# A residual block-attention kernel: the first tile of Wo transposed by VectorE in 32x32 blocks, two of its column quarters loaded through GpSimd's queue, with smaller units and a re-ranked plan

## The chip, the cores and the metric

One core of a Trainium2 chip runs the whole program. The metric is the device time in microseconds of one execution; the median of three is 150.2 us (149.64 to 150.42). The profile shows one of the executions (149.81 us), whose span from the first to the last instruction is 148.0 us. Below, x "at 44.6" means 44.6 us after the start of that span. The engines are TensorE (PE), VectorE (DVE), ScalarE (ACT), GpSimd (POOL) and SyncE (SP), which issues nearly all the transfers.

## What is computed

The input x is (8, 512, 1024) float32. The reference, cut to what matters, with NUM_BLOCKS = 8:

```python
block_repr = inputs.reshape(B, n_blocks, block_size, H).sum(axis=2)
keys = jnp.einsum('bnh,kh->bnk', block_repr, Wk)
keys = keys / jnp.sqrt(jnp.mean(keys * keys, axis=-1, keepdims=True) + EPS) * rms_weight
attn = softmax(jnp.einsum('bnh,h->bn', keys, query_vectors[layer_idx]))
attended = jnp.einsum('bn,bnh->bh', attn, block_repr)
proj = jnp.einsum('bh,kh->bk', attended, Wo)          # one vector for each batch element
y = inputs + proj
out = x + layernorm(y) * ln_gamma + ln_beta           # x is the same array as inputs
```

Each of the 8 batch elements has 512 rows of 1024 numbers. Their block sums pass through Wk to scores, the scores through a softmax to weights, and the weighted block sums through Wo to one vector, which is added to all 512 rows. Every row is then normalised, scaled, shifted and added to its input. 16.8 MB of x come in and as much goes out; the two weights are 4 MB each.

## The kernel before, in words

**Groups, rows and units.** The batch is worked in four groups of two elements (`GROUPS`). A group has four x tiles of 128 partitions by two rows by 1024 (1 MB each), eight "rows" (128x1024) in all; the program has 32 rows, 0 to 31. Rows are gathered into units (`UNITS`), and a unit shares one set of statistics.

**The start.** The weights come as four 1 MB tiles each, in the order of `LOADS` (k for Wk, x, o for Wo). TensorE transposes each tile with 16 matmuls against the identity (L400, two groups of eight, tile `pt`), and ScalarE copies the result from PSUM into `wkT` or `woT` (L407). The products of the first group with Wk and Wo are done quarter by quarter as the weight tiles arrive (L448, `first_keys`, `first_values`). Keys give the softmax weights through a chain of short operations on ScalarE, VectorE and TensorE (L571 to L617). The last step is the "spread" (L504 for the first group, L654 for the others): it puts the projected vector of each batch element on all partitions, in PSUM tile `pb`.

**A row's way.** y: VectorE adds `pb` to the row in place and sums it (L705). sq: ScalarE squares it with an accumulated sum (L713). When a unit's squares are there, GpSimd makes rs, the reciprocal deviation, and the statistics (L727, L728, L732, and L737 where a row is on VectorE). TensorE turns the statistics (pl, L742), and ScalarE or VectorE copies them to `lt` (L749; `LT_ACT` lists the units that ScalarE takes). For most rows ScalarE makes A = gam*rs + 1 (L762) and GpSimd multiplies the row by it (v, L767). For the rows in `ON_DVE`, TensorE makes that factor in PSUM (pA, L773) and VectorE multiplies (vd, L779). TensorE makes the additive part b from `lt` and `tab` (L794), VectorE adds it (out, L807), and SyncE stores the tile of two rows (L814).

**Order.** Nothing is scheduled at run time. Each step is handed to a `Plan` with an engine, an estimated cost, needs and a rank, and the plan simulates the engines and writes the instructions in the order of the simulated starts. The ranks `R` and the constants at the top decide that order; each engine then runs its list strictly in turn and waits where an operand or a buffer is missing. Buffers: 13 x tiles (`XBUFS`, shared with the weight tiles before they are transposed), two A tiles, two `lt`, one statistics tile, and single PSUM banks s1, s2, b0, b1 and pb.

Of the kernel before, what the change touches and what calls it, by code (L numbers as in the profile page):

```python
# [23 lines left out]
F32 = mybir.dt.float32  # L24
# [5 lines left out]
P = 128  # L30
# [2 lines left out]
NBLK = 8  # L33
GROUPS = (2, 2, 2, 2)
XBUFS = 13
ABUFS = 2
STATS = 1
LT_ACT = (1, 5, 7, 8, 9)

R = dict(  # L40
    y=3.0, sq=2.5, A=7.0, v=-6.0, out=0.5, vd=-1.0, scale=0.0, lt=-20.0, pl=-200.0, b=-250.0,
    pA=5.0, att=-10.0, hold=50.0, frac=0.8,
)
ON_DVE = (25, 27, 29, 31)
LOADS = "kxxxxkkkoooo"
W_DVE = ()
EV_DVE = ()
UNITS = (4, 4, 2, 4, 2, 4, 4, 4, 4)


class Plan:
# [4 lines left out]
    MB = 2.56  # L56
    LAND = 2.0
    BEGIN = 2.0

    def __init__(self, buffers):  # L60
        self.steps = []
        self.buffers = buffers

    def add(self, engine, cost, emit, needs=(), rank=0.0, moved=0.0, takes=None, gives=None):
        needs = [n for n in needs if n is not None]
        self.steps.append((engine, cost, emit, needs, rank, moved, takes, gives))
        return len(self.steps) - 1

# [45 lines left out]
    def emit(self):  # L114
        self.end, start, done = self.order()
        self.start, self.done = dict(enumerate(start)), dict(enumerate(done))
        for i in sorted(range(len(start)), key=lambda i: (start[i], i)):
            self.steps[i][2]()


@with_exitstack
def block_attn_resid_kernel(
# [11 lines left out]
    nc = tc.nc  # L134
    B, S, H = x.shape
    HC = H // P
    HALF = 512
    QU = H // 4
# [15 lines left out]
    ps = ctx.enter_context(tc.tile_pool(name="ps", bufs=1, space=bass.MemoryType.PSUM))  # L154
    ctx.enter_context(tc.manual_schedule())
    plan = Plan(dict(s1=1, s2=1, b=1, A=ABUFS, lt=2))
    for g in sizes:
        for n in range(STATS):
            plan.buffers[f"stat{g}_{n}"] = 1
# [115 lines left out]
    groups = []  # L275
    at = 0
# [12 lines left out]
    def load_w(which, s):  # L289
        def emit():  # L290
            if (which, s) in W_DVE:

                t = xp.tile([P, RT * 4, QU], F32, tag="x", name=f"w{which}_{s}")
                for j in range(4):
                    nc.sync.dma_start(out=t[32 * j : 32 * j + 32], in_=wq_v[which][s, :, :, bass.ts(j, QU)])
            else:
                t = xp.tile([P, RT, H], F32, tag="x", name=f"w{which}_{s}")
                nc.sync.dma_start(out=t, in_=w_v[which][s])
            stage[which, s] = t

        staged[which, s] = plan.add(SP, 0.5 if (which, s) in W_DVE else 0.35, emit, rank=-500 + len(loads), moved=1.0)

    def load_x(G, t, needs):
        def emit():
# [70 lines left out]
    def transpose_w(which, s):  # L375
        out_ = []
        if (which, s) in W_DVE:
            for c in range(0, HC, 2):
                def there_and_back(c=c):
                    t = stage[which, s].rearrange("p t (k c) -> p c t k", c=HC)  # L380
                    nc.vector.transpose(
                        (wkT, woT)[which][:, c : c + 2, bass.ts(s, QU)].rearrange("p c (t k) -> p c t k", k=32),
                        t[:, c : c + 2],
                    )

                out_.append(plan.add(DVE, 0.62, there_and_back, [staged[which, s]], -300 + which))
            halves[which, s] = out_
            frees.append(out_)
            return out_
        for h4 in range(HC // 4):  # L390
            n = turn[0]
            turn[0] += 1
            tag = ("b0", "b1", "pb")[n % 3] if n < 12 else ("b0", "b1")[n % 2]
            hold = {}

            def there(h4=h4, tag=tag, hold=hold):
                pt = ps.tile([P, 4, RT * P], F32, tag=tag, name=f"pt_{which}_{s}_{h4}")
                for c in range(4):
# [54 lines left out]
    def first_keys(G, T, columns, blkT):  # L453

        rank = -299.8
        parts = []
        for s in range(4):
            last = plan.add(PE, 0.97, lambda s=s: quarter(T, "keys", wkT, columns, s), [blkT, *halves[0, s]], rank, takes="s2")

            def e_part(s=s):  # L460
                if s == 0:
                    T["parts"] = chain.tile([P, 4, QU], F32, tag="parts", name="parts")
                nc.scalar.copy(T["parts"][:, s, :], T["po"])

            parts.append(plan.add(ACT, 0.37, e_part, [last], rank, gives="s2"))

        def e_keys():
            T["keys"]["po"] = ps.tile([P, QU], F32, tag="s1", name="keys0")
            for s in range(4):
                nc.tensor.matmul(T["keys"]["po"][32 * s : 32 * s + 32, :], diag4, T["parts"][:, s, :], start=True, stop=True)  # L470

        return plan.add(PE, 0.55, e_keys, parts, rank)

    def first_values(G, T, columns, share, blkT, rank):


        rank = -299.5
        T["w0"] = chain.tile([P, P], F32, tag="w", name="w0")

        def e_w0():  # L480
            nc.scalar.activation(T["w0"], weigh0, AF.Identity, scale=T["own"])
            T["pick"] = chain.tile([P, 2, P], F32, tag="pickw", name="pickw0")
            nc.scalar.activation(flat(T["pick"]), flat(pick0), AF.Identity, scale=T["own"])

        w0 = plan.add(ACT, 0.65, e_w0, [share], rank)
        vals = []
        for s in range(4):
            last = plan.add(
                PE, 0.97, lambda s=s: quarter(T, "values", woT, columns, s), [blkT, *halves[1, s]], rank, takes="s2"
            )  # L490

            def e_val(s=s):
                if s == 0:
                    T["val0"] = work.tile([P, 4, QU], F32, tag="A", name="val0")
                nc.scalar.copy(T["val0"][:, s, :], T["po"])

            vals.append(plan.add(ACT, 0.37, e_val, [last], rank, takes=None if s else "A", gives="s2"))
# [334 lines left out]
    for G in groups:  # L832
        attend(G)
        rows = [define_unit(u) for u, U in enumerate(units) if place[U["k0"]][0] is G]
        for _ in range(2):
            for unit_ in rows:
                next(unit_, None)
    plan.emit()
    return plan

# [29 lines left out]
```

## Time and profile before

| what | busy us | share of the span |
|---|---|---|
| TensorE matmuls | 122.6 | 83% |
| ScalarE | 101.2 | 68% |
| VectorE | 93.5 | 63% |
| GpSimd | 82.0 | 55% |
| the hardware queue of SyncE | | 70.2% of 16 DMA engines |

The shares are averages over stages with different limits. In the first third TensorE and the loads work and the other engines mostly wait; from 44.6 us on, VectorE, ScalarE and GpSimd share the rows. The costliest groups are v on GpSimd (28 of 2377 ns, 65.8 us), out (32 of 1216 ns, 38.2) and y (32 of 1213 ns, 37.6) on VectorE, sq (32 of 1143 ns, 36.6) and A (28 of 1142 ns, 31.8) on ScalarE. GpSimd's first statistic waits 47.0 us for its first squares. Page and trace name a line, an engine, an operation and the tiles written and read; in brackets stands the idle time of the engine just ahead, and what ended it.

### The profile page before, as it was taken

The page shows a single profiled execution, that of the slowest core. Times are in us where ns is not written, and L with a number is a line of the kernel's source. Part 1 is how long each engine was busy: PE and PEld are TensorE (multiplying, and loading weights), DVE is VectorE, ACT ScalarE, POOL GpSimd, SP SyncE. Part 2 cuts the span into 40 slices and gives each one's busy share as a digit, 9 for nine tenths or more (in the row PEclk, how much of TensorE's full clock was granted, in tenths as well). Part 3 has the DMA queues.
Part 4 walks back from the last instruction along what each step waited for, and adds up shares of the span by engine and source line. Part 5 has one row for each costly group of instructions (what it writes and reads, how often), then busy time and mean ns, then how long its engine had stood idle before and what let it go on. Part 6 is the DMA issues. An engine that isn't in the chain of part 4 may idle for free.

```text
span 148.0 us, 3021 instructions
## 1 busy us (share of the span) xinstructions
PE 122.6 (83%) x1176; PEld 66.2 (45%) x1176; DVE 93.5 (63%) x178; ACT 101.2 (68%) x160; POOL 82.0 (55%) x80
## 2 busy tenths in 40 slices
PE   0499989999999799969799999978894694998920
PEld 0465568768757344336354365425441212333400
DVE  6201010013109973769999899999797999694960
ACT  0352329678935999776999999998969999533000
POOL 7200000000000049999499999999999999978000
PEclk9999999999999999999999999999999555555555
DMA  4999999999999991258477795742562634657275
GB/s 131 437 408 425 398 408 411 410 415 422 416 414 418 421 403 38 106 206 354 190 248 317 292 361 210 288 193 91 213 263 91 279 133 164 283 210 301 91 317 215
DMA packets 6830, 42.15 MB, mean 285 GB/s; under 512 B 656, under 2 KB 672, under 8 KB 2720
## 3 DMA queue, kind: packets, MB, share of 16 engines
q1 hardware_dynamic: 6784, 41.95, 70.2%
q8 instruction: 9, 0.15, 0.4%
q14 instruction: 5, 0.04, 0.1%
q10 hardware_dynamic: 32, 0.02, 0.0%
HBM read 25.18 MB, written 16.78 MB: 283 GB/s over the span
## 4 chain that ended last, share of the span: by engine, by line
PE 44%; DVE 24%; issue 11%; ACT 8%; POOL 6%; DMA 3%; DVEq 1%; POOLq 0%; ACTq 0%
DVE x L705 14%; PE pt L400 12%; DVE x L807 8%; PE b L794 6%; POOL x L767 5%; PE pA L773 4%; ACT sq L713 4%; DMA w<-in_L_cond_Wk_dram 3%; ACT A L762 3%; PE bs L545 3%; PE keys L448 3%; PE values L448 3%; PE keys L433 3%; PE values L433 3%; PE pb L504 2%
## 5 line engine op out<-in xcount | busy, mean ns | idle before, releaser
L767 POOL TENSOR_TENSOR x<-x,A 128x1024 f32<-128x1024 f32 x28 | 65.8, 2377 | 4.8 <-ACT A L762 4.7
L705 DVE SCALAR_TENSOR_TENSOR x<-x,pb 128x1024 f32<-128x1024 f32 x32 | 37.6, 1213 | 7.1 <-PE pb L504 7.1
L807 DVE TENSOR_TENSOR x<-x,b 128x1024 f32<-128x1024 f32 x32 | 38.2, 1216 | 6.0 <-POOL x L767 5.3
L713 ACT ACTIVATE sq<-x,ysum 128x1024 bf16<-128x1024 f32 x32 | 36.6, 1143 | 2.5 <-DVE x L705 2.1
L794 PE MATMUL b<-tab,lt 32*128 32x512 f32 x128 | 33.1, 805 | 3.5 <-DVE x L807 2.7
L762 ACT ACTIVATE A<-gam,rs 128x1024 f32<-128x1024 f32 x28 | 31.8, 1142 | 5.8 <-POOL rs L728 3.5
L727 POOL TENSOR_SCALAR ssq<-ssq 128x4 f32<-128x4 f32 (+1 forms) x9 | 2.1, 228 | 48.2 <-ACT sq L713 47.7
L400 PE MATMUL pt<-ident,w 128*128 128x128 f32 x128 | 18.1, 299 | 5.9 <-DMA w<-in_L_cond_Wk_dram 5.9
L400 PEld LDWEIGHTS pt<-ident,w 128*128 128x128 f32 x128 | 16.5, 198 | 8.3 <-issue 8.3
L545 PE MATMUL bs<-x,blk 128*32 128x256 f32 x256 | 15.9, 386 | 1.4 <-issue 1.4
L794 PEld LDWEIGHTS b<-tab,lt 32*128 32x128 f32 x128 | 9.6, 226 | 16.3 <-DVE x L807 8.5
L433 PE MATMUL keys<-wkT,blkT 128*32 128x256 f32 x192 | 11.6, 382 | 2.3 <-DVE blkT L556 2.3
L433 PE MATMUL values<-woT,blkT 128*32 128x256 f32 x192 | 11.6, 381 | 0.5 <-ACT lt L749 0.5
L545 PEld LDWEIGHTS bs<-x,blk 128*32 128x32 f32 x256 | 7.7, 112 | 8.7 <-issue 4.2
L407 ACT COPY wkT<-pt 128x1024 f32<-128x1024 f32 x8 | 7.7, 1015 | 4.7 <-PE pt L400 4.7
L575 DVE SCALAR_TENSOR_TENSOR junk<-keys,qw 128x256 bf16<-128x256 f32 x4 | 1.7, 423 | 14.0 <-ACT junk L571 14.0
L773 PE MATMUL pA<-tabf,lt 32*128 32x512 f32 x16 | 8.1, 1108 | 2.4 <-DVE x L705 1.9
L407 ACT COPY woT<-pt 128x1024 f32<-128x1024 f32 x8 | 7.9, 1016 | 2.0 <-PE pt L400 2.0
L433 PEld LDWEIGHTS keys<-wkT,blkT 128*32 128x32 f32 x192 | 5.6, 109 | 8.0 <-DVE blkT L556 3.8
L728 POOL TENSOR_TENSOR rs<-ssq,power 128x4 f32<-128x4 f32 (+1 forms) x9 | 8.6, 961 | 0.8
L433 PEld LDWEIGHTS values<-woT,blkT 128*32 128x32 f32 x192 | 5.8, 110 | 4.9 <-issue 0.8
L779 DVE TENSOR_TENSOR x<-x,pA 128x1024 f32<-128x1024 f32 x4 | 4.9, 1221 | 3.1 <-PE b L794 3.1
(97 smaller groups left out, 112.5 us busy)
## 6 DMA issues: line engine op xcount, KB each, us to landing
x<-in_x_dram SPq DMA_DIRECT2D x16, 1024.0 KB, 14.1
out_dram<-x SPq DMA_DIRECT2D x16, 1024.0 KB, 4.1
w<-in_L_cond_Wk_dram SPq DMA_DIRECT2D x4, 1024.0 KB, 5.0
w<-in_L_cond_Wo_dram SPq DMA_DIRECT2D x4, 1024.0 KB, 19.4
gb<-in_cond_dram ACTq DMA_DIRECT2D x1, 4.0 KB
gb<-n_L_cond_rms_weight_dram ACTq DMA_DIRECT2D x1, 4.0 KB
gb<-in_L_cond_ln_gamma_dram ACTq DMA_DIRECT2D x1, 4.0 KB
gb<-in_L_cond_ln_beta_dram ACTq DMA_DIRECT2D x1, 4.0 KB
```

What stands on the lines that cost most here:

```text
L400: nc.tensor.transpose(pt[:, c, r * P : (r + 1) * P], stage[which, s][:, r, bass.ds(4 * h4 + c, P, step=HC)], ident)
L407: (nc.vector.tensor_copy if n in EV_DVE else nc.scalar.copy)(dst, hold["pt"])
L433: nc.tensor.matmul(hold["po"][32 * j : 32 * j + 32, :], lhs(c), wT[:, c, bass.ts(j, QU)], start=(c == 0), stop=(end and c == HC - 1),)
L448: nc.tensor.matmul(T["po"][32 * j : 32 * j + 32, :], columns(2 * j + c), wT[:, 2 * j + c, bass.ts(s, QU)], start=(c == 0), stop=(c == 1),)
L545: nc.tensor.matmul(T["bs"][32 * j : 32 * j + 32, :], blk[g], G["x"][t][:, r, bass.ts(j, QU)], start=(t == 0 and r == 0), stop=(t == G["til ...
L705: nc.vector.scalar_tensor_tensor(x_row(k), x_row(k), 1.0, G["pb"], ALU.mult, ALU.add, accum_out=U["sum"][:, i : i + 1])
L713: nc.scalar.activation(junk, x_row(k), AF.Square, bias=U["sum"][:, i : i + 1], scale=-float(H), accum_out=U["ssq"][:, i : i + 1],)
L762: nc.scalar.activation(U["A", k], gam, AF.Identity, bias=1.0, scale=U["rs"][:, k - k0 : k - k0 + 1])
L767: nc.gpsimd.tensor_tensor(x_row(k), x_row(k), U.pop(("A", k)), ALU.mult)
L773: nc.tensor.matmul(U["pA", k][:, i, :], U["lt"][lo : lo + 32, pair, :], tabf[lo : lo + 32, :], start=True, stop=True,)
L794: nc.tensor.matmul(U["b", pair][r][:, i, :], U["lt"][lo : lo + 32, pair, :], G["T"]["tab"][lo : lo + 32, :], start=True, stop=True,)
L807: nc.vector.tensor_tensor(x_row(k), x_row(k), flat(U["b", pair][k % RT]), ALU.add)
```

## The change

The stated aim is to take the first tile of Wo off TensorE. The tile is loaded in another layout, 32 partitions for each quarter of its columns, and VectorE transposes it in 32x32 blocks straight into `woT`. SyncE loads two of the quarters, GpSimd's queue the other two, which it issues once the second tile of Wk has landed. With it come: a third A buffer, paid for by letting `parts` use the buffers of `tab`; 13 units instead of 9; five rows on VectorE instead of four, spread over the program; eight units' `lt` on ScalarE instead of four units' in effect; other ranks; and a filler, a matmul whose result nobody reads, written into each gap that the plan sees on TensorE after the last group's spread. In the changed program there are 21 of them: runs of six, two, one, eight, and four single ones. An empty table of rank corrections (`NUDGE`) changes nothing.

```diff
-ABUFS = 2
+ABUFS = 3
-LT_ACT = (1, 5, 7, 8, 9)
+LT_ACT = (4, 6, 7, 8, 9, 10, 11, 12)
 R = dict(
-    y=3.0, sq=2.5, A=7.0, v=-6.0, out=0.5, vd=-1.0, scale=0.0, lt=-20.0, pl=-200.0, b=-250.0,
-    pA=5.0, att=-10.0, hold=50.0, frac=0.8,
+    y=2.0, sq=3.0, A=5.5, v=-3.0, out=-6.5, vd=-1.0, scale=-10.0, lt=10.0, pl=-20.0, b=-20.0,
+    pA=-250.0, att=-20.0, hold=1000.0, frac=1.0,
 )
-ON_DVE = (25, 27, 29, 31)
+ON_DVE = (10, 18, 27, 29, 31)
-W_DVE = ()
+W_DVE = ((1, 0),)
-UNITS = (4, 4, 2, 4, 2, 4, 4, 4, 4)
+UNITS = (2, 2, 4, 4, 4, 2, 2, 2, 2, 2, 2, 2, 2)
...
+            if self.steps[i][0] == "PE" and self.filler:
+                if at is not None:
+                    for _ in range(int((start[i] - at - 0.2) / self.FILL)):
+                        self.filler[1]()
+                if at is not None or i == self.filler[0]:
+                    at = done[i]
...
-                for j in range(4):
+                for j in range(2):
                     nc.sync.dma_start(out=t[32 * j : 32 * j + 32], in_=wq_v[which][s, :, :, bass.ts(j, QU)])
...
+        def others():
+            for j in range(2, 4):
+                nc.gpsimd.dma_start(
+                    out=stage[which, s][32 * j : 32 * j + 32], in_=wq_v[which][s, :, :, bass.ts(j, QU)]
+                )
+            i = plan.add(POOL, 2.0, others, [loads[len(loads) - 3], staged[which, s]], rank=-500)
...
-                out_.append(plan.add(DVE, 0.62, there_and_back, [staged[which, s]], -300 + which))
+                out_.append(plan.add(DVE, 1.07, there_and_back, [staged[which, s]], -300 + which))
...
-                    T["parts"] = chain.tile([P, 4, QU], F32, tag="parts", name="parts")
-                nc.scalar.copy(T["parts"][:, s, :], T["po"])
+                    T["parts", s // 2] = chain.tile([P, HALF], F32, tag="tab", name=f"parts{s // 2}", bufs=2)
+                nc.scalar.copy(T["parts", s // 2][:, bass.ts(s % 2, QU)], T["po"])
...
+    def e_fill():
+        idle = ps.tile([P, QU], F32, tag="s1", name="idle")
+        nc.tensor.matmul(idle, ident, gam[:, :QU], start=True, stop=True)
+    plan.filler = groups[-1]["spread"], e_fill
```

The branch for `W_DVE` is in the kernel before as well, but with an empty list nothing takes it. On the other engines the order moves with the ranks. In the changed program VectorE makes three of the four transposes, then the first group's dot product, then the fourth; TensorE takes Wo's second tile right after the first group's keys, and one block sum of the second group goes ahead of the first group's last spread matmul.

More of the change, by code (lines that the diff above doesn't have):

```diff
@@ L35 @@
 XBUFS = 13
-ABUFS = 2
+ABUFS = 3
 STATS = 1
-LT_ACT = (1, 5, 7, 8, 9)
+LT_ACT = (4, 6, 7, 8, 9, 10, 11, 12)
 R = dict(
-    y=3.0, sq=2.5, A=7.0, v=-6.0, out=0.5, vd=-1.0, scale=0.0, lt=-20.0, pl=-200.0, b=-250.0,
-    pA=5.0, att=-10.0, hold=50.0, frac=0.8,
+    y=2.0, sq=3.0, A=5.5, v=-3.0, out=-6.5, vd=-1.0, scale=-10.0, lt=10.0, pl=-20.0, b=-20.0,
+    pA=-250.0, att=-20.0, hold=1000.0, frac=1.0,
 )
-ON_DVE = (25, 27, 29, 31)
+ON_DVE = (10, 18, 27, 29, 31)
 LOADS = "kxxxxkkkoooo"
-W_DVE = ()
+W_DVE = ((1, 0),)
 EV_DVE = ()
-UNITS = (4, 4, 2, 4, 2, 4, 4, 4, 4)
+NUDGE = {}
+UNITS = (2, 2, 4, 4, 4, 2, 2, 2, 2, 2, 2, 2, 2)
 class Plan:
@@ L58 @@
     BEGIN = 2.0
+    FILL = 0.36
     def __init__(self, buffers):
@@ L62, in __init__ @@
         self.buffers = buffers
+        self.nudge, self.filler = {}, None
     def add(self, engine, cost, emit, needs=(), rank=0.0, moved=0.0, takes=None, gives=None):
         needs = [n for n in needs if n is not None]
+        rank += self.nudge.get(len(self.steps), 0.0)
         self.steps.append((engine, cost, emit, needs, rank, moved, takes, gives))
@@ L116, in emit @@
         self.start, self.done = dict(enumerate(start)), dict(enumerate(done))
+        at = None
         for i in sorted(range(len(start)), key=lambda i: (start[i], i)):
+            if self.steps[i][0] == "PE" and self.filler:
[4 more added lines that the diff above has]
+                    at = done[i]
             self.steps[i][2]()
@@ L156, in block_attn_resid_kernel @@
     plan = Plan(dict(s1=1, s2=1, b=1, A=ABUFS, lt=2))
+    plan.nudge = NUDGE
     for g in sizes:
@@ L299, in emit @@
             stage[which, s] = t
-        staged[which, s] = plan.add(SP, 0.5 if (which, s) in W_DVE else 0.35, emit, rank=-500 + len(loads), moved=1.0)
+        def others():
[3 more added lines that the diff above has]
+                )
+        staged[which, s] = plan.add(SP, 0.35, emit, rank=-500 + len(loads), moved=1.0)
+        if (which, s) in W_DVE:
+            i = plan.add(POOL, 2.0, others, [loads[len(loads) - 3], staged[which, s]], rank=-500)
+            staged[which, s] = plan.add("join", 0.0, lambda: None, [i, staged[which, s]])
     def load_x(G, t, needs):
@@ L460, in e_part @@
             def e_part(s=s):
-                if s == 0:
-                    T["parts"] = chain.tile([P, 4, QU], F32, tag="parts", name="parts")
-                nc.scalar.copy(T["parts"][:, s, :], T["po"])
+                if ("parts", s // 2) not in T:
+                    T["parts", s // 2] = chain.tile([P, HALF], F32, tag="tab", name=f"parts{s // 2}", bufs=2)
+                nc.scalar.copy(T["parts", s // 2][:, bass.ts(s % 2, QU)], T["po"])
             parts.append(plan.add(ACT, 0.37, e_part, [last], rank, gives="s2"))
@@ L469, in e_keys @@
             for s in range(4):
-                nc.tensor.matmul(T["keys"]["po"][32 * s : 32 * s + 32, :], diag4, T["parts"][:, s, :], start=True, stop=True)
+                nc.tensor.matmul(
+                    T["keys"]["po"][32 * s : 32 * s + 32, :], diag4, T["parts", s // 2][:, bass.ts(s % 2, QU)],
+                    start=True, stop=True,
+                )
         return plan.add(PE, 0.55, e_keys, parts, rank)
@@ L483, in e_w0, with e_val0 @@
             nc.scalar.activation(flat(T["pick"]), flat(pick0), AF.Identity, scale=T["own"])
+        def e_val0():
+            T["val0"] = work.tile([P, 4, QU], F32, tag="A", name="val0")
         w0 = plan.add(ACT, 0.65, e_w0, [share], rank)
+        val0 = plan.add("join", 0.0, e_val0, [blkT], rank, takes="A")
         vals = []
@@ L492, in e_val @@
             def e_val(s=s):
-                if s == 0:
-                    T["val0"] = work.tile([P, 4, QU], F32, tag="A", name="val0")
                 nc.scalar.copy(T["val0"][:, s, :], T["po"])
-            vals.append(plan.add(ACT, 0.37, e_val, [last], rank, takes=None if s else "A", gives="s2"))
+            vals.append(plan.add(ACT, 0.37, e_val, [last, val0], rank, gives="s2"))
         spread = None
```

## The prediction

> **What bounds the kernel now.** I read the 40 slices first, then busy time by stage, then VectorE's own timeline.
>
> ```profile
> PE   0499989999999799969799999978894694998920
> ...
> DVE  6201010013109973769999899999797999694960
> ...
> PEclk9999999999999999999999999999999555555555
> DMA  4999999999999991258477795742562634657275
> ```
>
> A slice is 3.7 us. TensorE is full from slice 5 to 12; then VectorE fills up and stays near 9 nearly to the end. TensorE's clock halves late.
>
> ```profile
> core 0: us, PE busy (x) PEld busy (x) DVE busy (x) ACT busy (x) POOL busy (x), PEclk, DMA share, GB/s
> 20.00:44.60 24.60, 24.60 (x253) 18.25 (x246) 2.21 (x13) 18.03 (x29) 0.00 (x0) 1.00 1.02 413
> 44.60:66.00 21.40, 18.57 (x249) 10.18 (x249) 15.78 (x34) 17.81 (x30) 12.13 (x10) 1.00 0.65 267
> 66.00:86.00 20.00, 19.23 (x245) 9.77 (x243) 19.39 (x39) 18.40 (x32) 17.70 (x14) 1.00 0.73 273
> 86.00:106.00 20.00, 17.94 (x227) 9.25 (x223) 19.14 (x38) 18.92 (x33) 19.51 (x14) 1.00 0.52 216
> 106.00:120.00 14.00, 9.78 (x42) 3.97 (x38) 12.77 (x17) 12.48 (x19) 13.75 (x9) 0.79 0.51 208
> 120.00:126.00 6.00, 3.85 (x13) 1.34 (x14) 5.98 (x9) 5.60 (x10) 5.67 (x7) 0.50 0.43 176
> 126.00:148.00 22.00, 15.22 (x50) 5.17 (x42) 13.91 (x12) 4.37 (x6) 9.58 (x8) 0.50 0.57 238
> ```
>
> From 20 to 44.6 TensorE is busy 24.6 of 24.6 us: weight transposes and the first group's products. Afterwards VectorE's column sums to 15.78 + 19.39 + 19.14 + 12.77 + 5.98 + 13.91 = 87.0 us. Its last operation ends at 143.0, so it idles 143.0 - 44.6 - 87.0 = 11.4 us; the last store takes the 5.0 us left. The span is therefore **44.6 (first spread) + 87.0 (VectorE work) + 11.4 (its idle) + 5.0 (tail) = 148.0**. Where the idle lies:
>
> ```profile
> 57.58 1.22 DVE L807 TENSOR_TENSOR x<-x,b 128x1024 f32<-128x1024 f32 x1 [2.81 <-POOL x L767]
> 66.02 1.22 DVE L807 TENSOR_TENSOR x<-x,b 128x1024 f32<-128x1024 f32 x1 [1.02 <-POOL x L767]
> 113.39 1.22 DVE L807 TENSOR_TENSOR x<-x,b 128x1024 f32<-128x1024 f32 x1 [1.04 <-POOL x L767]
> 127.18 1.22 DVE L779 TENSOR_TENSOR x<-x,pA 128x1024 f32<-128x1024 f32 x1 [1.19 <-PE b L794]
> 136.06 1.22 DVE L779 TENSOR_TENSOR x<-x,pA 128x1024 f32<-128x1024 f32 x1 [1.93 <-PE b L794]
> ```
>
> The brackets hold the wait before the row. By stage the idle is 5.6 us before 66.0 (VectorE waits for GpSimd's scaled rows), 1.5 from 66 to 106, 1.2 from 106 to 126, 3.1 from 126 to 143.0 (TensorE's b and pA at half clock).
>
> [...] the matmuls of b for one row (four records) take 1.13 us at 112.40 and 2.07 at 118.08; between lies a stretch from 110.7 to 114.7 with two short bursts. [...]
>
> **The change part by part.**
>
> *Startup.* TensorE loses the two groups of eight transposes of Wo's first tile: 2 x 1.09 us from the chain of waits = 2.2. ScalarE loses two copies of 1.01 us. VectorE gains four transposes of 128x512. [...] I take 0.9, 3.6 in all; VectorE is idle from 19.2 to 32.86, so they cost nothing if the tile is there. The queue moves about 410 GB/s; counting 1.05 MB tiles through the slices, Wo's first has landed at about 25.5 and the last at 33.5. GpSimd's two quarters wait for the second Wk tile (about 17.8). Their landing is [...] 14.1 at worst (the x row)[...]; I take 24. GpSimd itself idles until 51.59. Rows of 1 KB instead of 4 may add 0.5 us to the queue; Wo's last tile is wanted at 37, so that is hidden.
>
> Walking TensorE's new order from 28.15: without the two groups, Wk's last product waits about 0.5 us for its PSUM bank, and one block sum of the second group (1.0 us) now stands before the last spread. So the spread ends at 44.6 - 2.2 + 0.5 + 1.0 = 43.9; some of the sum fills the 0.3 us that the last spread already waited for a copy: **43.6**, a gain of 1.0.
>
> *Smaller units, third A buffer, new ranks.* Units go from 9 to 13, the first two of two rows. The first GpSimd statistic needs two squares, not four: it was at 51.59, 7.0 us after the spread; two squares (1.27 apart) fewer, less the tab copy now ahead of it, put it at +4.4. A new walk of the first stage gives v at +9.3, +12.9, +15.2, +17.6; the score and softmax lie between; the next group's spread is at +20.0 where it was at +22.5. Of the 5.6 us idle, **2.8** stay. GpSimd pays for more units: 0.23 + 0.71 + 0.21 = 1.15 us each of two rows against 1.47 of four. Ten and three: 15.9 us against 2 and 7: 12.6. Plus 3, less one product of 2.38: about 80 us of work from 48 to some 133, still below VectorE. ScalarE makes one A (1.14) less and four small copies (0.36) more, about even. The third A buffer removes waits that sum to 2.3 us on ScalarE, none on VectorE's path directly. Paying for it, parts shares tab's buffers: no time.
>
> *Rows on VectorE.* Five instead of four: +1.14 us, and -0.13 from lt copies moved to ScalarE: **88.0**.
>
> *Fillers.* 21 dead matmuls of 128x256 in the planned gaps after the last spread. The pgam and ptab rows give 0.43 to 0.53 us each at full clock, twice that at half; the plan allots 0.36. What is queued behind them is pl, pA and b, and VectorE waits for those. At full clock a run of eight overruns its gap by about 0.6 to 1.4 us, against three VectorE operations (3.4 us) queued ahead of the first pA consumer; hidden. If they hold the clock, b and pA shrink from about 2.07 to 1.13 us. With the two-row units at the end I leave **1.5** of the 4.3 us idle after 106, and for 66 to 106, with more units to pass, **2.0** instead of 1.5.
>
> Sum: 43.6 + 88.0 + (2.8 + 2.0 + 1.5) + 5.0 = 142.9, that is 5.1 below 148.0: 150.2 - 5.1 = **145.1 us**.
>
> **Rivals.**
> 1. *The quarters land late.* VectorE runs in order, and three transposes stand before the first group's dot product. Landing at 31.9 and three times 0.9 put the dot at 34.6, not 32.4; softmax weights and spread follow, +2.2: 147.3. For it: the queues are full then. [...]
> 2. *The clock halves anyway.* Fillers then take 0.86 us, the run of eight 6.9 us against about 3.1 planned, and pA comes 3.8 us late with 3.4 us of cover. The idle of the last stage stays at 4.3 and 0.6 is added: 145.1 + 3.4 = 148.5. For it: the plan's gaps are not the real ones.
> 3. *Slower: each unit exposes its round trip* (statistic, pl, lt, b), as the last units do now by 1.0 to 1.9 us. 13 x 1.1 = 14.3 idle, and no gain at the start: 44.6 + 88.0 + 14.3 + 5.0 = 151.9, so 154.1. For it: one stat tile, and GpSimd's columns at 19.51 of 20. Against: between 66 and 106 units pass with only 1.5 us idle.
> 4. *Better:* the first stage loses all but 1 us, the rest 2: idle 3.0, 141.8.
>
> **How the numbers follow.** Forecast 0.61 (143.3 to 146.9), late quarters 0.12, half clock 0.12, slower 0.08, better 0.07. The range 141.4 to 150.0 leaves out the slower case and the edges of the better and half-clock ones. Faster by over 0.5% (below 149.45): 0.86; same: 0.06, the upper end of half clock and late quarters; slower: 0.08.
>
> **What would show it.** First spread's end near 43.6; four transposes done before the dot at about 32.4; GpSimd's first statistic 4.4 us after the spread; second spread 20 us after the first; VectorE's work 88 us with idle near 6; clock at 1.00 after 114. It would be wrong if VectorE's transposes take over 2 us each, if GpSimd's share reaches 95% after its start, or if the wait ahead of pA grows at the end.

## The result, and the profile after

The changed kernel takes **154.67 us** (median of 4 runs, 153.88 to 156.56) against 150.1 for the kernel before (149.64 to 150.42). The ratio is **1.029**, with a 95% interval of 1.026 to 1.032: slower by 2.9%, where 145.1 us and a gain of 3.4% had been forecast. The profiled execution took 153.88 us, of which the span is 152.1. Executions of one kernel differ by 0.6 to 5.9 us, so the ratios compare only those within 1.5% of the quickest of their kernel, which leaves out 11 of the 20 executions of the first experiment below (median of all 150.6 us, against 150.0 for the kernel before).

First the 40 slices of the changed kernel (3.8 us each), three of the rows that were shown of the kernel before, and the one with the rate of the DMA queues:

```profile
PE   0498576988999989699995999988998999999900
DVE  7201010016530898886999976999999999939960
PEclk9999997899999999999999779999999999999985
GB/s 131 428 319 245 358 404 409 244 387 418 412 426 422 411 422 349 30 276 213 336 308 342 299 368 78 269 278 9 276 43 233 282 174 142 237 256 19 310 289 228
```

Two things in it contradict the forecast. The rate of the queues falls in the third and fourth slices (319, 245) and again in the eighth (244), where it should stay near 410. And TensorE, which was full from slice 5 to 12, shows 5, 7 and 6 in slices 5 to 7, with its clock lowered in slices 7 and 8. The right end looks as forecast but for one hole: the clock stays full until near the end, and VectorE stays full except in slice 36.

Busy time by stage of the changed kernel; the columns are the length of the stage, the busy time of TensorE's matmuls, its weight loads, VectorE, ScalarE and GpSimd with their counts, then clock, DMA share and GB/s:

```profile
20.00:44.60 24.60, 21.35 (x220) 15.80 (x224) 6.77 (x18) 13.73 (x23) 0.00 (x0) 0.93 1.04 383
44.60:66.00 21.40, 19.45 (x238) 11.35 (x230) 14.12 (x32) 17.29 (x31) 10.28 (x10) 1.00 0.80 333
66.00:86.00 20.00, 17.66 (x216) 9.07 (x212) 18.56 (x34) 17.49 (x29) 17.69 (x14) 1.00 0.86 285
86.00:106.00 20.00, 18.93 (x225) 9.21 (x227) 17.74 (x29) 16.52 (x26) 17.44 (x13) 0.92 0.54 220
106.00:126.00 20.00, 18.90 (x157) 8.84 (x149) 19.03 (x37) 17.37 (x34) 18.93 (x21) 1.00 0.50 204
126.00:153.00 27.00, 18.13 (x78) 7.39 (x76) 18.27 (x19) 10.80 (x17) 15.42 (x17) 0.90 0.48 199
```

VectorE's rows of the same kernel that start and end the forecast's sum, and the waits between (in brackets the idle time ahead of the row and what ended it):

```profile
50.13 1.22 DVE L733 SCALAR_TENSOR_TENSOR x<-x,pb 128x1024 f32<-128x1024 f32 x1 [6.05 <-PE pb L532]
...
69.93 1.22 DVE L733 SCALAR_TENSOR_TENSOR x<-x,pb 128x1024 f32<-128x1024 f32 x1 [1.23 <-PE pb L682]
...
92.62 2.35 DVE L835 TENSOR_TENSOR x<-x,b 128x1024 f32<-128x1024 f32 x2 [2.10 <-PE b L822]
...
136.41 1.22 DVE L807 TENSOR_TENSOR x<-x,pA 128x1024 f32<-128x1024 f32 x1 [2.60 <-PE b L822]
...
144.78 2.35 DVE L835 TENSOR_TENSOR x<-x,b 128x1024 f32<-128x1024 f32 x2 [0.17 <-PE b L822]
```

The first y starts at 50.1. VectorE's work after it is 14.12 + 18.56 + 17.74 + 19.03 + 18.27 = 87.7. Its last operation ends at 144.78 + 2.35 = 147.1, so it idles 147.1 - 50.1 - 87.7 = 9.3, and 5.0 are left for the last store. The equation of the prediction, filled in:

| term | before | forecast | measured |
|---|---|---|---|
| first spread | 44.6 | 43.6 | **50.1** |
| VectorE's work | 87.0 | 88.0 | 87.7 |
| its idle | 11.4 | 6.3 | **9.3** |
| tail | 5.0 | 5.0 | 5.0 |
| span | 148.0 | 142.9 | 152.1 |

Of the miss of 9.2 us, 6.5 lie in the start and 3.0 in the idle.

**The start.** TensorE, the transposes and the DMA issues of the changed kernel, in order of time:

```profile
4.52 1.43 POOL L316 DMA_DIRECT2D w<-in_L_cond_Wo_dram  x2
...
21.41 0.45 DVE L584 STREAM_TRANSPOSE blkT<-bs 128x256 f32<-128x256 f32 x1 [9.26 <-PE bs L573]
...
33.68 3.08 DVE L404 STREAM_TRANSPOSE woT<-w 128x512 f32<-128x512 f32 x3 [11.82 <-DMA w<-in_L_cond_Wo_dram]
...
35.94 1.16 PE L423 MATMUL pt<-ident,w 128*128 128x128 f32 x8 [0.50 <-DMA w<-in_L_cond_Wo_dram]
```

GpSimd issued its two quarters at 4.5 us, not after the second tile of Wk. The first group's block sums were complete (blkT) at 21.41; in the kernel before they were at 18.72. Busy time of the kernel before in stretches of 4 us, columns as above, and then of the changed kernel:

```profile
8.00:12.00 4.00, 4.00 (x36) 2.41 (x38) 0.12 (x1) 2.27 (x3) 0.00 (x0) 1.00 1.02 423
12.00:16.00 4.00, 4.00 (x48) 2.08 (x40) 0.30 (x1) 0.97 (x2) 0.00 (x0) 1.00 1.00 412
16.00:20.00 4.00, 3.34 (x47) 1.70 (x40) 0.45 (x1) 0.91 (x2) 0.00 (x0) 1.00 1.03 412
20.00:24.00 4.00, 4.00 (x40) 3.69 (x32) 0.00 (x0) 2.86 (x4) 0.00 (x0) 1.00 1.01 403
```

```profile
8.00:12.00 4.00, 4.00 (x40) 2.31 (x38) 0.28 (x1) 2.34 (x3) 0.00 (x0) 1.00 1.07 298
12.00:16.00 4.00, 3.36 (x28) 1.77 (x24) 0.14 (x1) 0.63 (x2) 0.00 (x0) 1.00 1.00 243
16.00:20.00 4.00, 2.13 (x20) 1.10 (x20) 0.00 (x0) 0.63 (x2) 0.00 (x0) 1.00 0.97 388
20.00:24.00 4.00, 2.14 (x32) 0.92 (x32) 0.45 (x1) 1.00 (x2) 0.00 (x0) 1.00 1.03 409
24.00:28.00 4.00, 3.72 (x18) 3.73 (x19) 0.00 (x0) 1.11 (x2) 0.00 (x0) 0.57 1.03 370
28.00:32.00 4.00, 3.88 (x42) 3.13 (x41) 0.00 (x0) 3.16 (x4) 0.00 (x0) 1.00 1.09 272
```

The queues carry 298 and 243 GB/s between 8 and 16 us, though their engines count as full (shares 1.07 and 1.00); the kernel before had 423 and 412 there. That is 1.2 MB less in 8 us, though GpSimd's two transfers are only 0.5 MB, and the block sums wait 2.7 us in all for x. TensorE then runs out of loaded data: 2.13 and 2.14 busy of 4.00 between 16 and 24, where it had 3.34 and 4.00. From 24 to 28 its clock is lowered, 0.57 on average. Between 28 and 32 the rate dips again, 272 against 410. The sum closes: from 12 to 40 us TensorE is busy 5.1 us less than before (22.2 against 27.3); at half clock for 3.4 us it loses another 1.7. 44.6 - 2.2 (the removed transposes) + 5.1 + 1.7 = 49.2. The remaining 0.9 is about what the new plan starts late without the Wo move (45.6 in the first experiment); that the two are the same is not shown.

**The end.** The run of eight fillers in the timeline of the changed kernel (x16: the program's 21 fillers left 42 records), and the groups of fillers and of VectorE's transposes (count, then busy time and mean ns of one, then the idle time before and its releaser):

```profile
129.24 6.00 PE L869 MATMUL idle<-gam,ident 128*128 128x256 f32 x16
```

```profile
L404 DVE STREAM_TRANSPOSE woT<-w 128x512 f32<-128x512 f32 x4 | 4.2, 1084 | 11.8 <-DMA w<-in_L_cond_Wo_dram 11.8
L869 PEld LDWEIGHTS idle<-gam,ident 128*128 128x128 f32 x42 | 6.3, 190 | 9.6 <-PE idle L869 6.6
```

Eight fillers take 6.0 us, 0.75 each, and the second group says why: the weight load of a filler is held by the filler before it (`<-PE idle`). Each takes a new PSUM tile from one buffer. VectorE's work ahead of it ends at 133.82, and it then waits 2.60 us for the next row with pA, at 136.41, because b and pA stand behind the fillers, which end at 135.24.

The chain that ended last names the two suspects at its head:

```profile
DMA w<-in_L_cond_Wo_dram 12%; DVE x L733 11%; PE idle L869 8%; PE b L822 8%; DVE x L835 8%; PE values L456 6%; SPq L308 6%; PE pt L423 4%; DMA gb<-in_L_cond_ln_beta_dram 4%; PE values L471 3%; PE keys L456 2%; PE pb L682 2%; ACT A L790 2%; PE pA L801 2%; PE bs L573 2%
```

Loads of Wo are 12% of it and fillers 8%. A chain shows one path; what each suspect costs was measured.

### The profile page after: what moved, and what is told of

Read it like the earlier page. It is cut to its first block, busy times and chain, and to the rows that moved or that the text cites. A ratio compares the mean times of both kernels' runs of the same rounds, so it can differ in the third digit from the quotient of the medians.

```text
span 152.1 us, 3107 instructions
## 1 busy us (share of the span) xinstructions
PE 125.9 (83%) x1206; PEld 68.9 (45%) x1206; DVE 98.4 (65%) x183; ACT 98.1 (65%) x161; POOL 84.8 (56%) x96
## 4 chain that ended last, share of the span: by engine, by line
PE 43%; DVE 22%; DMA 16%; SPq 6%; ACT 4%; issue 4%; DVEq 1%; ACTq 1%; POOL 0%; POOLq 0%
DMA w<-in_L_cond_Wo_dram 12%; DVE x L733 11%; PE idle L869 8%; PE b L822 8%; DVE x L835 8%; PE values L456 6%; SPq L308 6%; PE pt L423 4%; DMA gb<-in_L_cond_ln_beta_dram 4%; PE values L471 3%; PE keys L456 2%; PE pb L682 2%; ACT A L790 2%; PE pA L801 2%; PE bs L573 2%
## 5 line engine op out<-in xcount | busy, mean ns | idle before, releaser
L795 POOL TENSOR_TENSOR x<-x,A 128x1024 f32<-128x1024 f32 x27 | 63.6, 2380 | 5.2 <-ACT A L790 5.2
L790 ACT ACTIVATE A<-gam,rs 128x1024 f32<-128x1024 f32 x27 | 30.5, 1143 | 3.9 <-POOL rs L756 3.6
L755 POOL TENSOR_SCALAR ssq<-ssq 128x2 f32<-128x2 f32 (+1 forms) x13 | 3.0, 227 | 49.1 <-ACT sq L741 48.1
L423 PE MATMUL pt<-ident,w 128*128 128x128 f32 x112 | 17.8, 323 | 7.8 <-DMA w<-in_L_cond_Wk_dram 7.2
L822 PE MATMUL b<-tab,lt 32*128 32x512 f32 x128 | 20.5, 638 | 0.4 <-DVE lt L777 0.3
L869 PE MATMUL idle<-gam,ident 128*128 128x256 f32 x42 | 14.5, 426 | 0.7
L404 DVE STREAM_TRANSPOSE woT<-w 128x512 f32<-128x512 f32 x4 | 4.2, 1084 | 11.8 <-DMA w<-in_L_cond_Wo_dram 11.8
L756 POOL TENSOR_TENSOR rs<-ssq,power 128x2 f32<-128x2 f32 (+1 forms) x13 | 10.2, 788 | 1.1
L869 PEld LDWEIGHTS idle<-gam,ident 128*128 128x128 f32 x42 | 6.3, 190 | 9.6 <-PE idle L869 6.6
L822 PEld LDWEIGHTS b<-tab,lt 32*128 32x128 f32 x128 | 5.9, 183 | 6.7 <-issue 2.4
L430 ACT COPY woT<-pt 128x1024 f32<-128x1024 f32 x6 | 6.0, 1014 | 3.0 <-PE pt L423 2.9
## 6 DMA issues: line engine op xcount, KB each, us to landing
w<-in_L_cond_Wo_dram POOLq DMA_DIRECT2D x2, 256.0 KB, 10.5
```

Source lines behind the costliest of these rows:

```text
L423: nc.tensor.transpose(pt[:, c, r * P : (r + 1) * P], stage[which, s][:, r, bass.ds(4 * h4 + c, P, step=HC)], ident)
L756: nc.gpsimd.tensor_tensor(U["rs"][:, :N], ssq, power[:, :N], ALU.pow)
L790: nc.scalar.activation(U["A", k], gam, AF.Identity, bias=1.0, scale=U["rs"][:, k - k0 : k - k0 + 1])
L795: nc.gpsimd.tensor_tensor(x_row(k), x_row(k), U.pop(("A", k)), ALU.mult)
L822: nc.tensor.matmul(U["b", pair][r][:, i, :], U["lt"][lo : lo + 32, pair, :], G["T"]["tab"][lo : lo + 32, :], start=True, stop=True,)
L869: nc.tensor.matmul(idle, ident, gam[:, :QU], start=True, stop=True)
```

## The experiments

The theory after the result: the loads of Wo's first tile make the loss, in two ways (GpSimd's start too early, and the quarters' form), and the rest of the change gains a little. The rivals: the new units and ranks are slower in themselves; the fillers cost more than they hold; VectorE's transposes are too slow; rows of 1 KB are slow.

**The change without the Wo move** (`e1_wo_on_tensore`).

```diff
-W_DVE = ((1, 0),)
+W_DVE = ()
```

> The changed kernel, but Wo's first tile loaded and transposed by TensorE as in the kernel before (W_DVE empty); units, ranks, buffers and fillers stay changed. Theory L (the loss is in the loading: the first spread ends at 50.1 instead of 44.6 because the quarters delay the loads): the first y starts at 44.5 to 46, VectorE's stretch from there keeps its 97 us, so about 149 us. Theory F (the fillers are the loss, the loads a side show): only a little better, 152 to 153 us, since later stages absorb an earlier start.

Measured: ratio to the kernel before 0.990 (0.987 to 0.993), so 1.0% faster by this measure. The first y is at 45.59, 4.5 us earlier than in the changed kernel. The Wo move costs 1.029 - 0.990, some 5.9 us. The new plan is not to blame, but its end keeps the wait behind the fillers, in VectorE's timeline of this run:

```profile
131.88 1.22 DVE L807 TENSOR_TENSOR x<-x,pA 128x1024 f32<-128x1024 f32 x1 [2.59 <-PE b L822]
```

**The change without fillers** (`e2_no_fillers`).

```diff
-    plan.filler = groups[-1]["spread"], e_fill
```

> The changed kernel without the 21 dead matmuls. Theory L: the start is unchanged (first y at 50.1) and the time is within 1 us of the changed kernel's 154.5, the more so if TensorE's clock now halves after the last spread and b and pA take twice as long. Theory F: the 2.6 us wait ahead of the first pA consumer disappears and nothing comes instead, about 151.5 to 152 us.

Measured: 155.0 us, the median of four (152.44 to 156.21), and no ratio: inconclusive. Its profile shows the clock at half from 124.5 to the end (mean 0.50 from 126 on), and in place of the one wait of 2.6 us several for b and pA.

**The new plan alone, without the Wo move and without fillers** (`e5_tensore_no_fillers`): both edits above together.

> The kernel of e1 (Wo's first tile back on TensorE) without the dead matmuls. In e1 they run one after another at 0.75 us each, eight of them ahead of the pA that VectorE then awaits for 2.6 us. If fillers are only a cost: the 2.6 us go, about 146.5 us. If they pay for what they cost: TensorE's clock halves after about 115, the pairs of b take 2.1 us again, and the waits for b and pA near the end sum to about 3 us as in the kernel before: 148 to 149 us, level with e1.

Measured: ratio 1.0005 (0.997 to 1.004), clock at half from 115.8 (mean 0.75 from 106 to 126 us). The units, ranks and the third A buffer alone change nothing that can be measured. By these ratios the 1% of the first experiment comes from the fillers, even one after another: about 1.6 us net. The medians of all runs differ less, 150.6 with fillers and 150.9 without.

**All four quarters through SyncE** (`e3_all_quarters_synce`).

```diff
-                for j in range(2):
+                for j in range(4):
                     nc.sync.dma_start(out=t[32 * j : 32 * j + 32], in_=wq_v[which][s, :, :, bass.ts(j, QU)])
...
-            for j in range(2, 4):
-                nc.gpsimd.dma_start(
-                    out=stage[which, s][32 * j : 32 * j + 32], in_=wq_v[which][s, :, :, bass.ts(j, QU)]
-                )
+            pass
```

> The changed kernel with all four quarters issued by SyncE, in line with the other loads; GpSimd's queue moves nothing. The plan's order is the same. If GpSimd's queue is the culprit (it starts at 4.5 us and takes its half megabyte ahead of x): the block sums' transpose is back at 18.7 from 21.4, the first spread near 47, about 151.5 us. If the short rows of the quarters are the culprit whoever issues them: the block sums are on time, but the four quarters now all stand in SyncE's line, Wo's tiles land as late as in the changed kernel, first y at 49 to 50, 154 us.

Measured: ratio 1.014 (1.005 to 1.023), first y at 49.29. The block sums are complete at 18.44 again, so GpSimd's transfers had delayed them. But now the queue drops to 204 GB/s from 24 to 28 us, at a DMA share of 1.17, and TensorE waits for Wo's second tile, in its timeline:

```profile
32.55 1.97 PE L420 MATMUL pt<-ident,w 128*128 128x128 f32 x8 [2.99 <-DMA w<-in_L_cond_Wo_dram]
```

Its eight transposes take 1.97 us, against 1.16 at full clock (35.94 above): after the wait TensorE is at half clock (the mean from 20 to 44.6 us is 0.86, and 1.00 in the first experiment). Both parts of the theory hold.

**GpSimd held until the second Wk tile is there** (`e4_gpsimd_gated`). GpSimd copies one column of that tile ahead of its transfers.

```diff
+            mark = const.tile([P, 1], F32, tag="mark", name="mark")
+            nc.gpsimd.tensor_copy(mark, stage[0, 1][:, 0, 0:1])
             for j in range(2, 4):
```

> The changed kernel with a one-column GpSimd copy out of the second Wk tile ahead of GpSimd's two transfers, so that they really start only when that tile has landed, as the plan assumes; in the changed kernel nothing holds them and they start at 4.5 us. If the early start is the culprit: block sums at 18.7, first y at 46 to 47, 150.5 to 151.5 us. If the amount of slow traffic counts and not its moment: the quarters land later than now, VectorE's transposes move from 33.7 to 34 or later, first y at 49 to 50, 154 us.

Measured: ratio 1.0024 (0.9998 to 1.005). Timeline of this run:

```profile
17.49 0.45 DVE L586 STREAM_TRANSPOSE blkT<-bs 128x256 f32<-128x256 f32 x1 [6.38 <-PE bs L575]
18.56 0.19 POOL L316 COPY mark<-w 128x1 f32<-128x1 f32 x1 [13.99 <-DMA w<-in_L_cond_Wk_dram]
...
28.00 2.54 PE L425 MATMUL pt<-ident,w 128*128 128x128 f32 x16 [2.71 <-DMA w<-in_L_cond_Wk_dram]
...
48.07 1.22 DVE L735 SCALAR_TENSOR_TENSOR x<-x,pb 128x1024 f32<-128x1024 f32 x1 [6.04 <-PE pb L534]
```

The transfers now start at 18.7 instead of 4.5, and by the ratios 4.0 us are back (1.029 to 1.002). In the two profiles it is 3.2 us: the first y comes 2.1 earlier (50.13 to 48.07), and VectorE idles 1.7 less between 66 and 106, where this execution has no stretch at half clock (mean 1.00). So the early start costs 2.1 us in the first spread; whether it also brings on the later stretch is not shown. The rest, 1.2% above the first experiment, or 2.5 us in the first y, is the other part: the quarters fall among Wk's tiles, and TensorE waits 2.71 us for one of them.

**A later gate** (`e10_gated_third_wk`): the same copy from `stage[0, 2]`, the third tile of Wk. The first figures below are for two queues that move more side by side than one after the other.

> The changed kernel with GpSimd's two transfers held until the third Wk tile has landed (e4: the second), so that they run beside SyncE's two quarters, which go to the other half of the partitions. [...] TensorE's wait for Wo's second tile falls below 1.5 us and the first y comes at 46.5 to 47.5 (e4: 48.1); fast runs near 149 us. If only the sum of slow traffic counts: as e4, first y at 48, 150.5 us.

Measured: ratio 1.016 (1.010 to 1.023), first y at 51.15: worse than the earlier gate, and neither expectation holds. TensorE's waits for Wk after its first tile shrink from 3.8 us to 1.6, but Wo's second tile is late (timeline of this run):

```profile
34.43 1.97 PE L425 MATMUL pt<-ident,w 128*128 128x128 f32 x8 [3.67 <-DMA w<-in_L_cond_Wo_dram]
```

The busy time by stretch tells the two gates apart. With the earlier one the two queues together move 222 GB/s from 24 to 28 us, at a share of 1.08, hardly more than four quarters in a row through SyncE (204 in the same stretch of `e3_all_quarters_synce`), and 351 from 28 to 32. With the later one they move 296 and then 249 GB/s, at shares of 1.08 and 1.05, so the slow stretch falls later, ahead of Wo's second tile. The second queue gained hardly any rate. The quarters' time in the queue was moved but not hidden.

**What in the quarters is slow.** Two kernels leave the Wo tile on TensorE and change only how it is loaded. In `e8_short_rows_tensore` four column quarters go into all 128 partitions in rows of 1 KB:

```diff
-                nc.sync.dma_start(out=t, in_=w_v[which][s])
+                if (which, s) == (1, 0):
+                    for j in range(4):
+                        nc.sync.dma_start(out=t[:, :, bass.ts(j, QU)], in_=w_v[which][s][:, :, bass.ts(j, QU)])
```

> The kernel of e1, Wo's first tile still transposed by TensorE, but loaded in four transfers of 256 columns each, so in rows of 1 KB instead of 4. If the short rows are what costs time at the start (1024 bytes take 85 ns where 4096 take 168 to 175 in the records of before and after): the queue loses about 3 us, Wo's tiles land that much later, the first y moves from 45.6 to about 48, and the time is 1.5 to 2.5 us above e1. If the change's start is slow for another reason (VectorE's transposes, or TensorE left without work): as e1, first y at 45.6.

Measured: ratio 0.990 (0.986 to 0.993), the same as the first experiment; 49 ns for a packet of 1 KB in the DMA records, and TensorE is busy 23.94 of the 24.60 us from 20 to 44.6 (23.91 in the first experiment). The first y of its profile is late, but so were the block sums, which need no tile of Wo:

```profile
20.59 0.45 DVE L588 STREAM_TRANSPOSE blkT<-bs 128x256 f32<-128x256 f32 x1 [7.53 <-PE bs L577]
...
47.36 1.22 DVE L737 SCALAR_TENSOR_TENSOR x<-x,pb 128x1024 f32<-128x1024 f32 x1 [7.96 <-PE pb L536]
```

TensorE's first matmuls ran longer in this execution (up to 20 us it was busy 13.41 us with 104 records, in the first experiment 13.34 with 128). From block sums to first y it is 26.8 us, against 45.59 - 17.89 = 27.7. Short rows are not the cause. In `e9_partition_quarters` the rows keep 4 KB, and each of the four transfers fills 32 partitions (the line in the loop, the rest as in the edit above):

```diff
+                        nc.sync.dma_start(out=t[32 * j : 32 * j + 32], in_=w_v[which][s][32 * j : 32 * j + 32])
```

> The kernel of e1 (TensorE transposes Wo's first tile), with that tile loaded in its usual layout and rows of 4 KB, but in four transfers of 32 partitions each. e8 showed that rows of 1 KB into all 128 partitions take 49 ns, against 85 ns into 32. If writing only 32 partitions at a time is what slows the quarters: the 256 packets of these four transfers take about 300 ns or more each instead of 168, the queue moves 200 to 300 GB/s for 4 to 5 us, Wo's tiles land 2 us later or more, the first y moves from 45.6 to 47 or later. If neither is the cause (then the wide stride between rows of the column quarters is left): 168 ns, as e1.

Measured: ratio 1.004 (1.002 to 1.007), 1.4% above the first experiment. Busy time from 24 to 28 us in the first experiment, and in this one:

```profile
24.00:28.00 4.00, 4.00 (x51) 2.80 (x49) 0.00 (x0) 3.31 (x5) 0.00 (x0) 1.00 1.03 410
```

```profile
24.00:28.00 4.00, 3.88 (x48) 2.59 (x47) 0.00 (x0) 3.15 (x5) 0.00 (x0) 1.00 1.06 213
```

The queue moves 213 GB/s instead of 410 at a full share, and a packet of 4 KB takes about 330 ns (an estimate: 16 engines x 1.06 x 4.00 us, over the 208 packets that 213 GB/s make in that time) instead of 168. Then TensorE waits (timeline of this run):

```profile
30.03 1.14 PE L427 MATMUL pt<-ident,w 128*128 128x128 f32 x8 [1.92 <-DMA w<-in_L_cond_Wo_dram]
```

Thirty-two partitions at a time is the cause of the halved rate, 213 / 410 = 0.52; neither VectorE nor row length is in this run. By what mechanism is not shown.

**The Wo move on the old plan** (`e12_before_dve_tile`), the kernel before with one edit, which takes all four quarters through SyncE:

```diff
-W_DVE = ()
+W_DVE = ((1, 0),)
```

> The kernel before, all its plan, with only Wo's first tile given to VectorE through the branch it already has (four quarters by SyncE, no GpSimd queue, no fillers). If the move by itself loses through its load: TensorE waits some 3 us for Wo's second tile, first y at 46.5 to 48, later stages take the same 98 us, 152 to 153.5 us. If the loss in the changed kernel comes from the new plan instead: 148 to 150 us.

Measured: ratio 1.024 (1.020 to 1.027). Timeline and one stretch of busy time of this run:

```profile
33.87 1.36 PE L400 MATMUL pt<-ident,w 128*128 128x128 f32 x8 [3.09 <-DMA w<-in_L_cond_Wo_dram]
```

```profile
24.00:28.00 4.00, 3.07 (x35) 2.33 (x33) 0.00 (x0) 2.34 (x4) 0.00 (x0) 1.00 1.15 205
```

TensorE, rid of 2.2 us of transposes, waits 3.09 us for the next tile; the first y is at 48.66, 4.0 late. The loss needs neither GpSimd's queue nor the new plan. It is 1% more than the slow load cost in `e9_partition_quarters`. A stretch of 3.4 us at half clock (1.7 us lost), which follows the wait here and not there (mean clock from 20 to 44.6 us 0.93, against 1.00), would account for that; this was not tested by itself.

**The fillers' form.** `e6_fillers_075` (first experiment, and the plan counts 0.75 us per filler, so that eight fit in the gaps):

```diff
-    FILL = 0.36
+    FILL = 0.75
```

> The kernel of e1 with the filler's planned cost at 0.75 us instead of 0.36, which leaves eight fillers instead of 21. If the overrun of the run of eight is what VectorE waits for: the wait ahead of the first pA consumer falls from 2.6 to under 0.5 us and the clock still stays up, about 2 us below e1's own runs (146 to 147 us). If the 2.6 us have another cause (lt, or the rows): no change, 148 to 149 us.

Measured: ratio 1.0035 (0.999 to 1.008), so the expectation failed. The wait ahead of pA shrinks to 1.11, but the clock halves at 125.0 to 128.4 and from 135.2 (mean 0.66 from 126 on): eight fillers, the last at 129.9, do not hold it. `e7_one_filler_tile` (first experiment, all fillers into one PSUM tile, 19 of them):

```diff
-    FILL = 0.36
+    FILL = 0.43
...
-        idle = ps.tile([P, QU], F32, tag="s1", name="idle")
+        if "idle" not in vec:
+            vec["idle"] = ps.tile([P, QU], F32, tag="s1", name="idle")
+        idle = vec["idle"]
```

> The kernel of e1 with all fillers writing one PSUM tile, so that none waits for the one before, and a planned cost of 0.43 us (19 fillers). If each filler's 0.75 us come from waiting for the last one's end: fillers now take about 0.43 us each, the run of seven some 3 us, and the wait ahead of pA falls below 1 us: 146 to 147.5 us. If 0.75 us is the matmul's own price: nothing changes.

Measured: ratio **0.983** (0.978 to 0.988), 147.91 us median: faster than both kernels, the best version found. Timeline of this run:

```profile
125.76 3.29 PE L871 MATMUL idle<-gam,ident 128*128 128x256 f32 x14
...
130.58 1.22 DVE L807 TENSOR_TENSOR x<-x,pA 128x1024 f32<-128x1024 f32 x1 [0.25 <-PE b L822]
```

Seven fillers take 3.29 us, so 0.47 each from the first to the last record, where eight had taken 6.0; the wait of 2.59 falls to 0.25. The interval still touches that of the first experiment (up to 0.993), so the size of this gain is less sure than the wait's end.

**Gate and filler tile together** (`e11_repaired`): the change with the later gate, the one filler tile and its planned cost of 0.43, edits as shown above.

> The kernel of e10 with the fillers on one PSUM tile and a planned cost of 0.43 us, as in e7: the change with both faults mended. If moving Wo's first tile to VectorE is worth something once its load is cheap: below e7's 147.9 (0.983 of before), near 146.5. If TensorE merely waits for the next tile instead of transposing, so that the move is worth nothing or less: level with e7 at best, 148 to 149.5 us.

Measured: ratio 1.009 (1.007 to 1.012), first y at 49.77, TensorE's wait for Wo 3.66; the median of 151.85 us is above even the second expectation. Next to 0.983 without the Wo move, the move costs 2.6% with this gate. The earlier gate had done better (1.002 against 1.016) and was not run with the one filler tile, so 2.6% is not the least that the move can cost; the 1.2% between the earlier gate and the first experiment is an estimate of that.

## Why the prediction was wrong

**Failed: "Rows of 1 KB instead of 4 may add 0.5 us to the queue ... so that is hidden."** This is the error that no gate removes. The length of the rows was costed, the number of partitions was not. The 0.5 us was the author's estimate; the packets of `e8_short_rows_tensore` give about as much, (4 x 49 - 168) ns x 256 / 16 = 0.45 us for the tile. In the kernel's time, rows of 1 KB cost nothing that could be measured (0.990 with them and without); 32 partitions at a time halve the queue for 1 MB, 410 to about 210 GB/s, and everything behind is some 2.5 us later (1 MB at 410 is 2.6 us, at 205 it is 5.1). "Wo's last tile is wanted at 37" looked at the wrong tile: the second tile is wanted as soon as TensorE has lost the work on the first. With the quarters through SyncE, the 2.2 us removed turned into a wait of 3 (2.99, and 3.09 on the old plan), then a stretch at half clock. In the changed kernel itself this wait is 0.50, because TensorE had already lost its time to x and Wk.

**Failed: "GpSimd's two quarters wait for the second Wk tile (about 17.8) ... I take 24."** They started at 4.52. A need in the plan only orders what is written into an instruction list; the transfer carries no wait for that tile, and GpSimd's list has nothing else early on (its last operation before, L278, starts at 4.48). With the copy in front the issue is at 18.68. The walk of the program's need was taken for a wait on the chip. Cost: 4.0 us by the ratios with and without the gate, 2.1 of them in the first spread. The 24 for the landing was the author's estimate, since no run had shown GpSimd's queue carrying data; in the changed kernel the two landed 10.5 us after their issue (median). In its trace the one queue held the other up: x and Wk fell behind, at 298 and 243 GB/s between 8 and 16 us, while the share stood at 1.07 and 1.00; with all quarters through SyncE the block sums are complete at 18.44 again.

Together these put the startup term at 50.1 instead of **43.6**: 2.0 us are the gain that did not come (45.6 without the Wo move), 2.5 the quarters' form and 2.1 the early start. The four VectorE transposes themselves were hidden: 1084 ns each against the 0.9 taken, an estimate of the author's (twice blkT's 447 ns for half the columns would be 0.89).

**Failed in part: "At full clock a run of eight overruns its gap by about 0.6 to 1.4 us ... hidden."** The rows of ptab and pgam gave 0.43 us, but these do not wait for one another. With a new tile for each out of one PSUM buffer a filler takes 0.75, so eight overrun by 6.0 - 3.1 = 2.9 us. The 3.4 us of cover were not there: VectorE was done at 133.82 and waited 2.60, and a growing wait ahead of pA was the prediction's own sign of being wrong. (Rival 2 has 0.6 where 3.8 - 3.4 gives 0.4.) The idle after 106 is 0.97 + 2.86 = 3.8, not 1.5.

**Failed: idle of 2.0 from 66 to 106.** It is 1.44 + 2.26 = 3.7. Most is the wait of 2.10 at 92.62: the clock halves for 3.4 us at 86, and a group of values took 5.08 us there, where the keys of the same shape had taken 3.66. In the profiles of `e4_gpsimd_gated` and `e11_repaired`, which have no such stretch, this idle is 2.05, as forecast. No run says why the clock halves there in some executions and not in others.

**Right.** VectorE's work, 87.7 (88.0). The second spread 19.8 us after the first (20.0). The first stage's idle: 66.0 - 50.1 - 14.1 = 1.8, better than 2.8. GpSimd's first statistic at 54.00, so +3.9 (+4.4). The clock at full after 114, until 147. TensorE's clock as the reason of the fillers: without them it is at half from 115.8 (`e5_tensore_no_fillers`), with 21 of them it is full from 89.4 to 147.4. What halves it is not shown: the two stretches at half clock in the changed kernel that end before the program does, from 24.5 and from 86.0, last 3.41 us each, and in the 3.41 us before the first TensorE was busy 1.54. But the gain of all this was 1%, not 3.4, and without fillers nothing.

**The rivals.** Late quarters was right in direction and put at +2.2; its path was another. GpSimd's quarters were early. SyncE's two, and the tiles around them, were late, but VectorE's dot product did not wait for the transposes: three of them ended at 36.8, and the dot started at 38.55, after the keys. The slower case (each unit exposes its round trip) gave 154.1 and is right in number only: from 66 to 106 the units leave 3.7 us idle, most of it in one wait of another cause.

**What stays open.** With GpSimd's half megabyte beside x, the queues moved 1.2 MB less between 8 and 16 us, more than the 0.5 MB that half a rate for those bytes alone would cost; why is not shown. The earlier gate with one filler tile was not run, and neither was the Wo tile in VectorE's layout without the halved rate. The lone effect of the fillers beside the Wo move (`e2_no_fillers`) is not settled either.

## What to carry to other kernels

In a stage bound by loading, work taken off the engine that consumes the loads turned into a wait here (2.2 us of transposes into 2.99 and 3.09 us), so price any change to the form of a transfer for everything queued behind it: look at GB/s beside the DMA share, since the sign of it here was 213 GB/s instead of 410 at a share of 1.06. A need in a scheduler that writes instruction lists is no wait on the chip (the transfers were issued at 4.52, not after 17.8); find the semaphore or the operand that holds a transfer. Dummy matmuls that keep the clock up did best here on one shared PSUM tile (0.983 against 0.990), and their number counts: with 19 the mean clock from 126 us on was 0.86, with eight 0.66.

## What had not been expected of the hardware

- A load into 32 partitions at a time runs at 204 to 213 GB/s with the DMA engines counted as full (shares of 1.06 to 1.17), against 410 into 128 (1.03); a packet of 4 KB takes about 330 ns by the estimate above, instead of 168. With two of the quarters on each queue the two move 222 GB/s together (24 to 28 us with the earlier gate).
- Rows of 1 KB into 128 partitions take 49 ns each, about 17% more per byte than rows of 4 KB (168); into 32 partitions, on SyncE's queue, 85 (the mean in the changed kernel).
- A VectorE transpose of 128x512 fp32 from SBUF to SBUF takes 1084 ns, 2.4 times the 447 of 128x256 out of PSUM.
- With eight fillers between 117 and 130 us TensorE's clock was at half from 125.0 and again from 135.2 (mean 0.98 from 106 to 126 us, 0.66 from 126 on); with 19 between 117 and 138 the means were 1.00 and 0.86. The clock also halved at 24.5 us in the changed kernel, where the longest gap after the first matmul was 1.84 us and TensorE was busy 2.13 and 2.14 of 4 us in the two stretches before.
